# A conv and attention block in f32: position terms out of the first pair's front, second filters' steps held behind the first attention, cv1 and m2 ahead of the second projection

## The chip, the cores and the metric

The kernel runs on one core of a Trainium2 chip. The core has five engines that run side by side, each with its own list of instructions: PE (matmuls), DVE (VectorE, elementwise work), ACT (ScalarE, activations and copies), POOL (GpSimd, small elementwise work here and the issue of stores) and SP (which only issues DMA transfers, mostly loads). An engine takes its list strictly in order; an instruction that waits for a semaphore holds up everything behind it on the same engine. The metric is device time of one execution in microseconds, and the median over several executions is given.

## The reference

Eight images of 512 channels on 32 x 32 positions, all in float32. The block is a group norm, a 1x1 convolution, two bottleneck layers with a 3x3 convolution and self-attention, and a closing 1x1 convolution with a residual:

```python
def bot_attention(x, qkv_w, rw, rh):          # x: b, 256, 32, 32
    qkv = conv2d(x, qkv_w, 0).reshape(b, 3, HEADS, HD, hw)
    q, k, v = (qkv[:, 0], qkv[:, 1], qkv[:, 2])
    r = (rw + rh).reshape(1, HEADS, HD, hw)
    logits = jnp.einsum('bhdi,bhdj->bhij', q, k + r) * HD ** (-0.5)
    a = jax.nn.softmax(logits, axis=-1)
    return jnp.einsum('bhij,bhdj->bhdi', a, v)
...
t = cbs(x, cv1_w, cv1_bn, 0)                  # 1x1, 512 -> 512, BN, silu
ys = [t[:, :C], t[:, C:]]                     # y0, y1: 256 channels each
for i in range(N):                            # N = 2 layers
    yi = ys[-1]
    z = cbs(yi, m_cv1_w[i], m_cv1_bn[i], 1)   # 3x3
    z = bot_attention(z, m_qkv_w[i], m_rw[i], m_rh[i])
    z = silu(bn_eval(conv2d(z, m_cv2_w[i], 0), m_cv2_bn[i]))   # "m2"
    ys.append(yi + z)
return cbs(jnp.concatenate(ys, axis=1), cv2_w, cv2_bn, 0)
```

The input is group-normalised (32 groups) before this block, and the input is added to its result. The position term r is a sum of one vector per column (rw, 256 x 32) and one per row (rh, 256 x 32): 256 channels by 1024 positions once it is spread out. HD is 64, there are 4 heads.

## The kernel before

**Tiling and order.** Channels lie on partitions, 128 at a time (NM = 2 blocks for 256 channels, NX = 4 for 512), positions on the free axis in halves of 512. The images are taken in four pairs. For each pair: group norm and cv1 of both images, 3x3 convolution of layer 1 for both, then projection and attention of the first image, a transition in which the next image's cv1, the first image's m2 and the second image's projection are done, the attention of the second image, and the same again for layer 2; then cv2. Each pair also does the next pair's norm and cv1 in the shade of its attentions and transitions. Pair 0 multiplies the 1x1 layers plainly (`project_direct`, `conv1x1`), later pairs use Strassen blocks that pair 0 prepares.

**The 3x3 convolution** works on transformed tiles. `tiles_in` turns an image into v_in on DVE (w_ba, w_ec, w_rows, w_d, w_ab on the way), `conv3x3` multiplies them with transformed filters u, and the result is turned back. A filter for a block of output channels oc and of input channels k is made by `make_u`: raw taps are loaded (576 KB) into a spare image buffer (`load_raw`, tile ypad) or into `taps` (`load_taps`), then in three rounds DVE forms row sums in place (L406 to L412) and six u_new tiles per round (L424 to L429), ACT two more (L422, L423), and POOL stores them to DRAM (L433). `make_u` is a generator: each `next` takes one of its eight steps. The u_new tiles come from small rings of buffers (six for the early ones, ten for the late), so a step waits until an earlier store has landed. Layer 1's filters are made in the front; those of layer 2 are named (0,0,0) ... (1,1,1) by (oc, k, spare buffer). (0,0,0) is stepped behind the first attention, (0,1,1), (1,0,1), (1,1,1) after it: 16 steps ahead of the second attention, eight hooked into it (`hooks(NORM_B, range(8, 16), ...)`), which between them make the 24 steps.

**The front of pair 0** (about 0 to 135 us) loads and normalises two images, makes layer 1's filters and cv1 of both images, then v_in of both images for three rounds i (L528 to L575), then the convolution. A few matmuls make the position term: `make_r_early(0)` lets PE spread rw and rh with a unit matrix (L205, L208, tile r_ps), ACT copies it (L214), and SP stores it (tile r). `project_direct` loads it again (r_in, L811) and adds it to the keys when they leave PSUM (kr, L822). For layer 2 the same term is made by `make_r(1)` on POOL (L218 copy, L222 add, L226 store).

**The transition** between pair 0's attentions (224 to 303 us). On PE: cv1 of the next pair's first image (ps<-x,w: 8 matmuls for each of four output blocks; blocks 0 and 1 first), first half of the second image's projection (ps<-z,w_qkv: k and q), s_ps (the sums of the last softmax group over partitions, L1024), v of the projection (L833), m2 of the first image (m_ps, L1205), remaining cv1 blocks, second half of the projection. The softmax sums of the last group take a way round: s_ps on PE, s_row on ACT, a DRAM round trip by SP into sums_all, rc on DVE (L1067), another round trip into rs, and z scaled by it on DVE (L1079); m2's last products need that z. cv1's blocks go through y_half or ypad on ACT (silu, L476), m2's through t.

**What sets the order.** Instructions stand on each engine in an order that is fixed when the kernel is built: a list scheduler weighs the data dependences and the order in which the code was written, and `with tc.issue_after(ins)` holds back all that is written inside until `ins` stands in the order. Work is handed to the attention as a table `behind` of callbacks, keyed by softmax group g or (g, step), which are called as the attention's steps are written; NG = 4 is the end. `end` holds what closes an attention: `end.added` (the last sum of probabilities), `end.sums`, `end.spread`, `end.scale`. PSUM tiles for 1x1 products come from a ring of three (`ps_big`), and one is free again when ACT or DVE has read it.

Of the kernel before, what the change touches and what calls it, by code (L numbers as in the profile page):

```python
# [44 lines left out]
F32 = mybir.dt.float32  # L45
I32 = mybir.dt.int32
AF = mybir.ActivationFunctionType
ALU = mybir.AluOpType
# [4 lines left out]
P = 128  # L53
# [8 lines left out]
def kernel(  # L62
# [63 lines left out]
        return yp[:, 1 : F + 1].rearrange("p h c w -> p (h c w)")  # L126

    def load_raw(n, oc, k, yp):
        nc.sync.dma_start(
            inside(yp)[:, : 9 * P].rearrange("p (t o) -> p t o", o=P), m_cv1_w[n, ts(k, P), :, ts(oc, P)]  # L130
        )
        return inside(yp)
# [59 lines left out]
    def load_m2(n):  # L192
        nc.sync.dma_start(m2_sb[:, n], m_cv2_w[n].rearrange("(k p) o -> p k o", p=P))

    def make_r_early(n, raw):

        for c in range(NM):
            nc.scalar.copy(planes(rw_sb[:, n, c : c + 1]), natural(raw[:, c : c + 1]))
        ident = act.tile([P, P], F32, tag="h", name="ident", bufs=2)
        make_identity(nc, ident)  # L200
        for c in range(NM):
            ps = ps_big.tile([P, NH, HALF], F32, tag="big", name="r_ps")
            for half in range(NH):
                to = ps[:, half, :].rearrange("p (h w) -> p h w", w=F)
                nc.tensor.matmul(  # L205
                    to, ident, rw_sb[:, n, c].unsqueeze(1).to_broadcast([P, ROWS, F]), start=True, stop=False
                )
                nc.tensor.matmul(  # L208
                    to, ident, rh_sb[:, n, c, ts(half, ROWS)].unsqueeze(2).to_broadcast([P, ROWS, F]),
                    start=False, stop=True,  # L210
                )
            for half in range(NH):
                r = act.tile([P, HALF], F32, tag="t", name="r_new", bufs=4)
                nc.scalar.copy(r, ps[:, half, :])  # L214
                nc.sync.dma_start(r_dram[n][c][:, ts(half, HALF)], r)

    def make_r(n, raw):
        nc.gpsimd.tensor_copy(planes(rw_sb[:, n]), natural(raw))  # L218
        for c in range(NM):
            for half in range(NH):  # L220
                r = act.tile([P, ROWS, F], F32, tag="t", name="r_new", bufs=4)
                nc.gpsimd.tensor_tensor(  # L222
                    r, rw_sb[:, n, c].unsqueeze(1).to_broadcast([P, ROWS, F]),
                    rh_sb[:, n, c, ts(half, ROWS)].unsqueeze(2).to_broadcast([P, ROWS, F]), ALU.add,
                )
                nc.gpsimd.dma_start(r_dram[n][c][:, ts(half, HALF)], r.rearrange("p h w -> p (h w)"))  # L226
# [245 lines left out]
    def stages(act, small, ps_big, ps_av, n_pt):  # L472
# [330 lines left out]
        def project_direct(n, z, w, early=None, middle=None):  # L803
# [5 lines left out]
            for c in range(NM):  # L809
                rs.append(act.tile([P, HW], F32, tag="pt", name="r_in", bufs=n_pt))  # L810
                nc.sync.dma_start(rs[c], r_dram[n][c])  # L811

            def qk(c):
                for which in (1, 0):
                    o = which * C + c * P
                    ps = conv1x1(
                        lambda k: w[k][:, o : o + P], lambda k, half: z[:, k, ts(half, HALF)], NM
                    )
                    if which == 0:
                        nc.scalar.copy(q[:, c], ps.rearrange("p a b -> p (a b)"))  # L820
                    else:
                        tt(kr[:, c], ps.rearrange("p a b -> p (a b)"), rs[c], ALU.add)  # L822

            qk(0)
            if early:
# [659 lines left out]
    def putter(vs, g):  # L1485
        return lambda i, cp: vs[i, cp][:, :, g]
# [91 lines left out]
    for p in range(NP):  # L1578
# [70 lines left out]
            next(norm, None) if norm else None  # L1649

        def step_u():
            next(more_u, None)

        def begin_cv1(which, y1, b):
            def run():
# [24 lines left out]
        if p == 0:  # L1680
            q_tiles = [act.tile([P, 3 * C], F32, tag=tag, name="qkv_raw") for tag in ("p3", "p4")]
            load_qkv(1, q_tiles)
            q_sums = [act.tile([P, 2, 3, P], F32, tag=tag, name="sq_new") for tag in ("p1", "p2")]
            before = behind[3, 2]
            behind[3, 2] = lambda: (before(), make_sq(1, q_tiles, [t[:, j] for t in q_sums for j in range(2)]))
        end = s.attention_fast(qkv, z[:, :, 0], at_of(ia, 0), behind)
        for made in more_u:
# [9 lines left out]
                nc.gpsimd.dma_start(v_dram[i][cp], v_new.pop((i, cp)))  # L1697

        ec = {}
        if p == 0:  # L1700
            more_u = filters([(0, 1, 1), (1, 0, 1), (1, 1, 1)])

        def m2_a():
            return s.m2(0, z[:, :, 0], Y1[0], lambda oc, half: inner(Y2[0], oc, half))
# [20 lines left out]
            feed(units(1)[:6])  # L1725
            qkv = s.project_strassen(0, z[:, :, 1], take_blocks("sq", 0, 1, SQ_NAMES), t)
        else:
            if p == 0:
                with tc.issue_after(end.added.ins):
                    make_r(1, load_r(1, "acc", 2))  # L1730
            else:
                t = s.first_sum(z[:, :, 1])
            if more:
                nxt.go_on()

            def middle():
                end.spread()
                end.scale()
                m2_a()
                if more:  # L1740
                    for i in range(2, 4):
                        nxt.rest(i)
                    nxt.keep()
                s.exp_table()

            if not more:
                feed(units(1)[:6])
            if direct:
                qkv = s.project_direct(
                    0, z[:, :, 1], [take(key) for key in direct_keys(1)], early=end.sums, middle=middle  # L1750
                )
# [8 lines left out]
            store(i)  # L1760

        norm = None
        if p == 0:
# [13 lines left out]
        def parts_of(ocs):  # L1777
# [24 lines left out]
        for made in more_u:  # L1802
            pass
        if more:
            nxt.sums()
        vs = v_units()
# [29 lines left out]
        if p == 0:  # L1836
# [197 lines left out]
```

## Time and profile before

| | us |
|---|---|
| runs | 2362.28, 2359.41, 2361.51 (median 2361.51) |
| profiled execution, its own time | 2363.26 |
| its span on the core | 2361.7 |
| PE busy | 2239.6 (95%) |
| DVE busy | 1741.9 (74%) |
| ACT busy | 1087.8 (46%) |
| POOL busy | 211.8 (9%) |
| mean granted PE clock | 0.987 |

The profile is of one execution. Its page divides the span into 40 slices of 59 us, with one digit per slice for the busy share in tenths. A timeline line gives start, duration, engine, source line, operation, output<-inputs, shape and how many instructions were drawn together; in brackets stands the idle time of the engine just before it and the operation that ended the wait. `[5.41 <-ACT y_half L476]` reads: the engine stood for 5.41 us, and what let it go on was ACT's y_half of line 476. "x8" on PE counts records; one f32 matmul of 128 x 512 leaves two and takes 0.859 us when rows of them follow each other (27.63 us for 64 records, x_second). A window line gives, for a stretch from:to, its length, the busy time and instructions of PE, PEld, DVE, ACT and POOL, the granted PE clock, the DMA engines' mean share and the GB/s. A share may come out a little over 1.

Where pair 0 lies in the span: front 0 to 135, first attention 158 to 224, transition 224 to 303, second attention 303 to 374, layer 2's convolution from 409, its first attention 464 to 522. Pair 1's first transition, 824.17 to 874.68, takes 50.5 us; pair 0's takes 78.9.

### The profile page before, as it was taken

To read this page: it belongs to the slowest core of one execution; us is meant where nothing else is said; L and a number is where in the kernel's file an instruction comes from. 1 tells how busy PE (TensorE), PEld (TensorE's weight loads), DVE (VectorE), ACT (ScalarE), POOL (GpSimd) and SP (SyncE) were. 2 spreads that over 40 slices of the span, in tenths; PEclk is the share of its full clock that TensorE was granted. 3 is DMA by queue.
4 is the path that set the end of the run, shared out by engine and by line. 5 is a ranking of instruction groups with operands and counts; after the bars stand their busy time and mean duration, and the time that the engine had idled before them with its cause. 6 is when DMAs were issued, how large, how long until landed. Compare 5 with 4: busy or idle time off the path is not lost.

```text
span 2361.7 us, 40480 instructions
## 1 busy us (share of the span) xinstructions
PE 2239.6 (95%) x16354; PEld 1086.2 (46%) x16354; DVE 1741.9 (74%) x2626; ACT 1087.8 (46%) x1325; POOL 211.8 (9%) x416
## 2 busy tenths in 40 slices
PE   7798799999999999999999999999999999999997
PEld 3553333734447343744346444463344733373443
DVE  5967477877947878986775868887794777787642
ACT  6244254355323666355422565635522354335532
POOL 3103211000021000000022001000002100000002
PEclk9899899999999999999999999999999999999999
DMA  9522633631257051523147233351126711161114
GB/s 319 205 102 88 213 110 129 223 105 49 68 152 249 23 174 55 177 91 104 33 121 233 100 98 105 101 188 60 64 68 151 244 33 59 57 202 33 55 24 134
DMA packets 132930, 283.40 MB, mean 120 GB/s; under 512 B 34208, under 2 KB 60048, under 8 KB 131712
## 3 DMA queue, kind: packets, MB, share of 16 engines
q1 hardware_dynamic: 105712, 198.01, 25.7%
q0 software_dynamic: 27024, 82.72, 11.5%
q8 instruction: 131, 2.15, 0.4%
q14 instruction: 63, 0.52, 0.1%
HBM read 212.65 MB, written 68.03 MB: 119 GB/s over the span
## 4 chain that ended last, share of the span: by engine, by line
PE 54%; DVE 16%; issue 15%; DMA 5%; ACT 2%; POOL 1%; SPq 0%; DVEq 0%; ACTq 0%; POOLq 0%
PE av_ps L1007 13%; PE l_ps L973 12%; PE c L1225 5%; PE p_ps L863 5%; PE m_ps L1205 4%; PE c_new L1225 3%; PE x_ps L1325 3%; PE ps L502 2%; DVE acc L993 2%; PE c_ps L619 2%; DMA c_out<-in_x_dram 2%; PE pv_ps L869 2%; ACT pt L977 1%; DMA rs<-r_dram 1%; PE s_ps L1024 1%
## 5 line engine op out<-in xcount | busy, mean ns | idle before, releaser
L977 ACT ACTIVATE pt<-l_ps 128x1024 f32<-128x1024 f32 x512 | 495.7, 1023 | 345.9 <-PE l_ps L973 313.6
L993 DVE TENSOR_TENSOR acc<-acc,pt 128x1024 f32<-128x1024 f32 x384 | 471.9, 1229 | 90.1 <-ACT pt L977 66.8
L973 PE MATMUL l_ps<-q,kr 64*64 64x512 f32 x4096 | 490.9, 593 | 15.5 <-ACT pt L977 13.7
L1007 PE MATMUL av_ps<-pt,vT 64*64 64x512 f32 x4096 | 491.0, 597 | 10.2 <-DVE z L1015 7.9
L973 PEld LDWEIGHTS l_ps<-q,kr 64*64 64x64 f32 x4096 | 156.5, 133 | 289.6 <-issue 247.6
L1007 PEld LDWEIGHTS av_ps<-pt,vT 64*64 64x64 f32 x4096 | 155.8, 134 | 288.2 <-issue 240.0
L619 PE MATMUL c_ps<-v_in,u 128*64 128x128 f32 x4320 | 239.8, 273 | 5.5 <-issue 5.5
L619 PEld LDWEIGHTS c_ps<-v_in,u 128*64 128x64 f32 x4320 | 235.8, 137 | 13.1 <-issue 13.0
L1205 PE MATMUL m_ps<-z,m_sb 128*128 128x512 f32 x256 | 114.4, 600 | 3.5 <-DVE z L1079 3.5
L863 PE MATMUL p_ps<-t_z,sq 128*128 128x512 f32 x224 | 106.7, 597 | 7.8 <-DVE c_t L626 7.8
L991 DVE TENSOR_TENSOR acc<-pt 128x1024 f32<-128x1024 f32 x64 | 78.0, 1218 | 38.0 <-ACT pt L977 38.0
L624 ACT COPY c_m<-c_ps 128x512 f32<-128x512 f32 x48 | 28.1, 586 | 165.9 <-PE c_ps L619 105.2
L476 ACT ACTIVATE t<-m_ps,bh,sh 128x512 f32<-128x512 f32 x64 | 46.8, 775 | 98.7 <-PE m_ps L1205 98.3
L863 PE MATMUL p_ps<-z,sq 128*128 128x512 f32 x168 | 80.2, 604 | 8.2 <-ACT z L476 8.2
L1275 POOL DMA_DIRECT2D c_out<-in_x_dram x56 | 50.4, 975 | 310.4 <-ACT c_out L476 307.1
L1205 PEld LDWEIGHTS m_ps<-z,m_sb 128*128 128x128 f32 x256 | 48.6, 192 | 62.8 <-issue 54.6
L1079 DVE TENSOR_TENSOR z<-z,rs 128x512 f32<-128x512 f32 x64 | 44.8, 699 | 34.3 <-DMA rs<-r_dram 34.3
L537 POOL MEMSET w_rows<- 128x32 f32 x48 | 7.9, 164 | 649.6 <-PE s_ps L1024 377.0
L1015 DVE TENSOR_TENSOR z<-av_ps,z 128x512 f32<-128x512 f32 x64 | 43.9, 687 | 27.1 <-ACT z L1014 27.1
L476 ACT ACTIVATE z<-z,bh,sh 128x512 f32<-128x512 f32 x64 | 46.9, 803 | 30.1 <-DVE z L657 29.3
L476 ACT ACTIVATE c_out<-cz,bh,sh 128x512 f32<-128x512 f32 x14 | 16.7, 1293 | 91.1 <-DVE cz L1302 91.1
L863 PEld LDWEIGHTS p_ps<-t_z,sq 128*128 128x128 f32 x224 | 38.7, 190 | 39.9 <-issue 28.9
(313 smaller groups left out, 3200.0 us busy)
## 6 DMA issues: line engine op xcount, KB each, us to landing
u<-u SPq DMA_DIRECT2D x135, 512.0 KB
r_in<-r SPq DMA_DIRECT2D x32, 512.0 KB
sq<-sq SPq DMA_DIRECT2D x42, 384.0 KB
rs<-r_dram SPq DMA_DIRECT2D x120, 128.0 KB
x<-in_x_dram SPq DMA_DIRECT2D x28, 512.0 KB
y_in<-y SPq DMA_DIRECT2D x28, 512.0 KB
c_out<-in_x_dram POOLq DMA_DIRECT2D x56, 256.0 KB, 5.3
out_dram<-c_out POOLq DMA_DIRECT2D x56, 256.0 KB, 3.5
```

The costliest lines, as they stand in the source:

```text
L476: silued[0] = nc.scalar.activation(dst, src, AF.Silu, scale=sh[:, k : k + 1], bias=bh[:, k : k + 1])
L619: nc.tensor.matmul(to[o], us[cp][:, k, row, c, o], rhs, start=(k == 0), stop=(k == NM - 1),)
L863: nc.tensor.matmul(ps[:, o, :], w[:, o, :], rhs, start=not onto, stop=True, skip_group_check=onto)
L973: nc.tensor.matmul(ps[kh * HD : (kh + 1) * HD, hd, :], kr[r, c, o : o + HD], q[r, c, ts(half, HALF)], start=True, stop=True,)
L977: last_exp[0] = exp = nc.scalar.activation(pt, ps, AF.Exp, scale=SCALE)
L991: return nc.vector.tensor_tensor(accs[g], pt[0], pt[1], ALU.add)
L993: ins = nc.vector.tensor_tensor(accs[g], accs[g], pt[i], ALU.add)
L1007: nc.tensor.matmul(avs[g][hd * HD : (hd + 1) * HD, kh, :], vT[r, j, o : o + HD], pt[i][r, hd, :], start=(j == 0), stop=(j == NJ - 1),)
L1205: nc.tensor.matmul(pss[oc][:, half, :], m2_sb[:, n, k, ts(oc, P)], ao[:, k, ts(half, HALF)], start=(k == 0), stop=(k == NM - 1),)
L1225: nc.tensor.matmul(ps[:, o, :], w[:, k, ts(o, P)], rhs[part][:, c], start=(k == 0 and not onto), stop=(k == KB - 1), skip_group_check=onto,)
L1275: nc.gpsimd.dma_start(t, rows_of(x, i, at), accum_op=ALU.add)
L1325: nc.tensor.matmul(ps[:, o, :], w[:, c, ts(o, P)], rhs[c], start=(c == 0 and not onto), stop=(c == 1), skip_group_check=onto,)
```

## The change

1. The front no longer spreads layer 1's position term: `make_r_early` goes, and with it r_ps, the unit matrix, four ACT copies, four stores and the loads of r_in. `turn_r` only brings rw into its layout (two ACT copies). `project_direct` adds rw and then rh to the keys on DVE, broadcast from the small tiles.
2. The spread term of layer 1, which pair 1 needs, is made by POOL (`make_r(0, None)`) behind layer 2's first attention of pair 0. That of layer 2 (`make_r(1, ...)`) is written behind the first attention of layer 1 instead of after it.
3. `load_raw` for layer 2 is issued by POOL instead of SP.
4. In the front five steps of the filter (0,1) of layer 1, instead of two, stand ahead of the second image's averages.
5. The 24 steps of layer 2's filters (0,1,1), (1,0,1), (1,1,1) are held behind `end.added` of the first attention and all lie in the transition (5, 7, 3 and the remaining 9 steps, each part held behind the one before); none is hooked into the second attention.
6. The transition is written in another order for pair 0: sums, cv1 block 1, spread, steps, scale, m2, cv1 blocks 2 and 3, and only then the whole projection of the second image, so `early` and `middle` of `project_direct` are no longer used.

```diff
     def load_raw(n, oc, k, yp):
-        nc.sync.dma_start(
+        (nc.gpsimd if n else nc.sync).dma_start(
...
+    def turn_r(n, raw):
+        for c in range(NM):
+            nc.scalar.copy(planes(rw_sb[:, n, c : c + 1]), natural(raw[:, c : c + 1]))
...
-    def make_r_early(n, raw):
...
     def make_r(n, raw):
-        nc.gpsimd.tensor_copy(planes(rw_sb[:, n]), natural(raw))
+        if raw is not None:
+            nc.gpsimd.tensor_copy(planes(rw_sb[:, n]), natural(raw))
...
-            rs = []
-            for c in range(NM):
-                rs.append(act.tile([P, HW], F32, tag="pt", name="r_in", bufs=n_pt))
-                nc.sync.dma_start(rs[c], r_dram[n][c])
...
-                        tt(kr[:, c], ps.rearrange("p a b -> p (a b)"), rs[c], ALU.add)
+                        dst = img(kr[:, c])
+                        rw = rw_sb[:, n, c].unsqueeze(1).to_broadcast([P, F, F])
+                        rh = rh_sb[:, n, c].unsqueeze(2).to_broadcast([P, F, F])
+                        tt(dst, img(ps.rearrange("p a b -> p (a b)")), rw, ALU.add)
+                        tt(dst, dst, rh, ALU.add)
...
-    make_r_early(0, rw_raw)
     chunk = make_u(0, 1, 0, areas[0, 1, 0], new=u_new_early)
     with tc.issue_after(made.ins):
-        for _ in range(2):
+        for _ in range(5):
             made = next(chunk)
...
+    turn_r(0, rw_raw)
...
+            first = behind[1, 2]
+            raw_1 = load_r(1)
+            behind[1, 2] = lambda: (first(), make_r(1, raw_1))
...
-                with tc.issue_after(end.added.ins):
-                    make_r(1, load_r(1, "acc", 2))
...
             if direct:
-                qkv = s.project_direct(
-                    0, z[:, :, 1], [take(key) for key in direct_keys(1)], early=end.sums, middle=middle
-                )
+                more_u = filters([(0, 1, 1), (1, 0, 1), (1, 1, 1)])
+                end.sums()
+                nxt.go_on()
+                end.spread()
+                with tc.issue_after(end.added.ins):
+                    for _ in range(5):
+                        made = step_u()
+                with tc.issue_after(made.ins):
+                    end.scale()
+                    for _ in range(7):
+                        made = step_u()
+                last = m2_a()
+                with tc.issue_after(made.ins):
+                    for _ in range(3):
+                        made = step_u()
+                for i in range(2, 4):
+                    nxt.rest(i)
+                nxt.keep()
+                s.exp_table()
+                with tc.issue_after(made.ins), tc.issue_after(last.ins):
+                    for made in more_u:
+                        pass
+                feed(units(1)[:6])
+                qkv = s.project_direct(0, z[:, :, 1], [take(key) for key in direct_keys(1)])
...
-        if p == 0:
-            for _ in range(16):
-                step_u()
-            feed(units(1)[:6])
...
-        behind = hooks(NORM_B, range(8, 16), {1: lambda: tiles_later(2)}) | {
+        behind = hooks(NORM_B, (), {1: lambda: tiles_later(2)}) | {
...
-            behind[2] = lambda: make_sq(0, tiles, sums)
+            behind[2] = lambda: (make_sq(0, tiles, sums), make_r(0, None))
```

More of the change, by code (lines that the diff above doesn't have):

```diff
@@ L193, in load_m2 @@
         nc.sync.dma_start(m2_sb[:, n], m_cv2_w[n].rearrange("(k p) o -> p k o", p=P))
-    def make_r_early(n, raw):
-        for c in range(NM):
[L198 to L206, printed above, removed]
-                )
[L208 to L215, printed above, removed]
     def make_r(n, raw):
-        nc.gpsimd.tensor_copy(planes(rw_sb[:, n]), natural(raw))
+        if raw is not None:
+            nc.gpsimd.tensor_copy(planes(rw_sb[:, n]), natural(raw))
         for c in range(NM):
@@ L807, in project_direct @@
             vT = act.tile([P, NJ, C], F32, tag="v", name="vT")
-            rs = []
-            for c in range(NM):
-                rs.append(act.tile([P, HW], F32, tag="pt", name="r_in", bufs=n_pt))
-                nc.sync.dma_start(rs[c], r_dram[n][c])
             def qk(c):
@@ L1651, in step_u @@
         def step_u():
-            next(more_u, None)
+            return next(more_u, None)
         def begin_cv1(which, y1, b):
@@ L1699 @@
         ec = {}
-        if p == 0:
-            more_u = filters([(0, 1, 1), (1, 0, 1), (1, 1, 1)])
         def m2_a():
@@ L1727 @@
         else:
-            if p == 0:
-                with tc.issue_after(end.added.ins):
-                    make_r(1, load_r(1, "acc", 2))
-            else:
+            if not direct:
                 t = s.first_sum(z[:, :, 1])
-            if more:
-                nxt.go_on()
             def middle():
@@ L1739, in middle @@
                 m2_a()
[L1740 to L1743, printed above, removed]
                 s.exp_table()
@@ L1748 @@
             if direct:
-                qkv = s.project_direct(
-                    0, z[:, :, 1], [take(key) for key in direct_keys(1)], early=end.sums, middle=middle
-                )
+                more_u = filters([(0, 1, 1), (1, 0, 1), (1, 1, 1)])
[22 more added lines that the diff above has]
+                qkv = s.project_direct(0, z[:, :, 1], [take(key) for key in direct_keys(1)])
                 feed(cv1_keys(1))
@@ L1762 @@
         norm = None
-        if p == 0:
-            for _ in range(16):
-                step_u()
-            feed(units(1)[:6])
         tiles_later(1)
@@ L1801 @@
         end = s.attention_fast(qkv, z[:, :, 1], at_of(ib, 0), behind, at_once=True)
-        for made in more_u:
-            pass
         if more:
```

## The prediction

> **What bounds the kernel now.** I read the busy slices first, then a table of stretches, then PE's timeline inside the stretches that look thin.
>
> ```profile
> PE   7798799999999999999999999999999999999997
> PEclk9899899999999999999999999999999999999999
> ```
>
> Each digit is 59 us. PE is full from the seventh slice on; only the first six (0 to 354 us, pair 0) have room, and the granted clock dips in the same ones. All parts of the change lie there, so the rest of the 2361.7 us is left alone.
>
> ```profile
> 158.07:224.22 66.15, 59.85 (x546) 21.19 (x545) 52.73 (x71) 42.20 (x51) 14.96 (x19) 0.97 0.13 46
> 224.22:303.13 78.91, 62.01 (x156) 29.60 (x152) 40.05 (x85) 21.07 (x31) 19.01 (x36) 0.89 0.66 228
> 303.13:373.73 70.60, 62.19 (x546) 20.47 (x545) 55.59 (x79) 41.16 (x48) 7.39 (x14) 0.95 0.21 74
> 766.02:824.17 58.15, 57.68 (x546) 21.54 (x545) 49.73 (x65) 39.15 (x44) 3.68 (x5) 1.00 0.08 24
> 874.68:937.46 62.78, 58.12 (x546) 20.18 (x545) 54.37 (x72) 39.14 (x44) 4.04 (x8) 1.00 0.12 39
> ```
>
> Columns: stretch, length, busy PE, PEld, DVE, ACT, POOL, clock, DMA share, GB/s. Rows one to three are pair 0's first attention, the transition, and its second attention; the last two are pair 1's attentions, the same matmuls without filter steps: 8.0 and 7.8 us shorter.
>
> In the front (0 to 135 us) the last wait is not PE's own:
>
> ```profile
> 54.01 0.56 DVE L406 TENSOR_TENSOR ypad<-ypad 128x384 f32<-128x384 f32 x1 [10.57 <-DMA ypad<-in_m_cv_w_dram]
> ...
> 96.93 5.54 PE L619 MATMUL c_ps<-v_in,u_new 128*64 128x128 f32 x64 [5.87 <-DVE v_in L574]
> 110.03 9.30 PE L619 MATMUL c_ps<-v_in,u_new 128*64 128x128 f32 x128 [7.57 <-ACT c_m L624]
> ```
>
> PE waits for v_in, which DVE makes without a gap from 60 to 140 us (9.4 to 9.97 of each 10 us). DVE is late because it stood 10.57 us for the raw taps of filter (0,1,1), which layer 2 alone needs. **DVE bounds the front.**
>
> In the transition PE waits four times, 16.9 us together:
>
> ```profile
> 247.07 5.58 PE L502 MATMUL ps<-z,w_qkv 128*128 128x512 f32 x8 [5.41 <-ACT y_half L476]
> 258.49 1.08 PE L1024 MATMUL s_ps<-acc,ones 128*32 128x256 f32 x8 [5.84 <-ACT y_half L476]
> 261.71 8.55 PE L833 MATMUL p_ps<-w_qkv,z 128*128 128x256 f32 x32 [2.14 <-DVE kr L822]
> ...
> 281.50 3.68 PE L1205 MATMUL m_ps<-z,m_sb 128*128 128x512 f32 x4 [3.50 <-DVE z L1079]
> ```
>
> The first two are PSUM waits on ACT, which stands behind u_new copies waiting for DVE filter steps. The last ends the chain of softmax sums: s_ps at 258.49, z at 280.75, 22 us.
>
> **Front: the position terms and the held steps.** PE loses 8 r_ps matmuls, 42.25 to 49.13: 6.88 us. It is hidden today behind DVE, but brings the second image's cv1 forward, which must happen for DVE to profit. ACT loses four copies of 0.52 us, SP four r stores and two r_in loads of pair 0's first projection. DVE loses the 10.57 us stall and the three 0.56 us operations behind it (1.65 us): 12.2. Against that, its next steps need u_new buffers; their stores take 8.8 us (512 KB) to land at a DMA share of 1.06, so I estimate 2.6 us of new waits. Image 0's first w_ba moves from 70.26 to about 60.5. Image 1's w_ba needs its last silu (71.65 + 2.28 = 73.93, less 6.88 = 67.05) and follows image 0's 7.48 us of tiles at 68.0: from 77.74, 9.7 earlier. So v_in, and the conv behind it, come about 9.7 us earlier; PE is ready at 85.35 - 6.88 = 78.5. PE alone would give 6.9, DVE alone 12.2 - 2.6 = 9.6.
>
> Against it stands something the words of the change don't say: in the changed instruction order POOL makes r(1) here, among the u stores (source: behind the first attention), and the broadcast adds meet DVE's busiest stretch. The row for this is at the end of the first attention today:
>
> ```profile
> 215.41 3.44 POOL L222 TENSOR_TENSOR r_new<-rw_sb,rh_sb 128x512 f32<-128x512 f32 x2
> ...
> 216.41 1.54 DVE L1079 TENSOR_TENSOR z<-z,rs 128x512 f32<-128x512 f32 x1
> 217.87 1.26 DVE L424 TENSOR_TENSOR u_new<-ypad 128x256 f32<-128x256 f32 x1
> 219.97 4.62 DVE L993 TENSOR_TENSOR acc<-acc,pt 128x1024 f32<-128x1024 f32 x2
> ```
>
> Alone these take 0.69, 0.42 and 2.56: 3.8 us lost. The Trainium skill (SBUF — State Buffer, "Who interferes with whom") says why, and speaks against the move: a DVE instruction with two SBUF inputs and a GpSimd one that reads SBUF exclude one another, and the later one waits for the whole instruction. By the rule DVE could lose all of POOL's 3.44 + 2.06 + 1.26 (copy) = 6.8 us; by the row 3.8, and some of the front's DVE operations have one input. I take 2.2. Front: 9.7 - 2.2 = **7.5** (5 to 10.6).
>
> Load_raw of layer 2 moves from SP to POOL: two loads among the front's u stores, two in the transition. A DMA issue costs POOL 0.54 us; the same page's box on DMAs from GpSimd warns that DVE can starve them, but POOL's 256 KB u stores land in 5.4 us in this front, beside a busy DVE. By the row it costs nothing as long as the u stores behind it aren't waited for; at worst the 2 us that they would slip, in the range above.
>
> **First attention.** The r_new contention leaves: the 3.8 us on DVE were mostly slack, PE idles there 1 to 2 us a time. Gain **1** (0 to 3).
>
> **Transition.** PE's new order: cv1 8 matmuls, s_ps, cv1 8, m2 6, cv1 1 group, m2's rest, cv1, then the whole projection. Bare work: 56 matmuls of 0.859 us = 48.1, v 7.1, s_ps 0.6: 55.8 us, so at most 78.9 - 55.8 = 23 can go. s_ps starts at T0 + 7 instead of T0 + 34. Pair 1 does the same chain, uncongested, from s_ps 827.73 to z 839.64 in 12 us; today's took 22, at a DMA share of 0.96. PE needs the scaled z at about T0 + 21. In between, the filters: all 24 steps now lie here (16 before), on DVE (per filter 18 operations at 0.34 and six at 0.6 us from issue to issue: 9.7) 29 us, and rc stands on DVE behind the first operation of filter (1,0,1), which waits for its raw load on POOL. That load can start when filter (0,1,1) has read its taps (T0 + 15), lands 5 to 6 us later, rc follows at about T0 + 22 to 25, rs 5 us after (the 4.97 us row): z at T0 + 27 to 30, a PE wait of 6 to 9. With 2 us for the clock and PSUM waits: 55.8 + 7.5 + 2 = 65.3. Gain 13.6, taken as **13** (5 to 17; the lower end if ACT's y_half waits of 5.4 and 5.8 stay, since cv1's second and third group still need PSUM from an ACT that also copies u_new). The kr adds double to two of 1.2 us on DVE for each c; in the first projection DVE has 1.42 us of work from 140 to 145 and almost none to 155, and the q products run behind k's; in the transition they follow all m2 work: nothing, or 1.2 if DVE's steps run late.
>
> **Second attention.** Its 8 hooked steps leave. Today 70.60 with 8.4 us of waits; pair 1's row without steps is 62.78. Gain **7** (4 to 7.8).
>
> **r(0).** POOL now makes it behind layer 2's first attention (463.92 to 522.19, 58.27 us); by the row above 3.8 us of DVE there, in an attention with 10 us of DVE slack: cost **1** (0 to 3). It is first needed by pair 1.
>
> **Sum:** 7.5 + 1 + 13 + 7 - 1 = 27.5. The profiled execution took 2363.26 us, its span 2361.7; the median of the other runs, 2361.51, is within 0.1% of either. 2361.5 - 27.5 = **2334**.
>
> **Rivals.** (a) The front's gain is taken elsewhere: DMA is at 1.03 to 1.06 from 20 to 50 us, and if the u stores, not the raw load, are what DVE meets next, the stall is only renamed. For: a 5.08 us u wait exists at 249.87. Against: the stores after 52 us landed with DMA at 0.65. Then 20 us remain: **2342**.
> (b) The packed steps make DVE the transition's bound: 29 us of steps, some 20 of sq, z, m2, tiles, kr and statistics, two load waits of 6 and the u wait of 5 already seen come to 66, and it starts 5 us behind and ends in kr: 71 to 75 us. Transition gain 4, front 6.5, rest 7: 17 us, **2345**; with y_half's waits repeated, 2348.
> (c) Slower: the raw load stalls rc. In the front such a load took 37.2 to 54.0, 16.8 us. At that price z comes at T0 + 41, the transition is 78 us and gives nothing. The other gains are 14.5 us, so the kernel loses once z comes after T0 + 56: the load would also have to stand 15 us in POOL's queue behind u stores that wait for ACT. Two such waits: **2367**.
> (d) The change doesn't do what it says: r(1) isn't behind the attention but in the front, where by the rule (6.8) instead of the row it takes the front's gain to 3: **2339**.
>
> **Numbers.** Forecast 0.55; a 0.13, b 0.18, c 0.05, d 0.09. The low end takes the upper bound of each part (10.6 + 3 + 17 + 7.8: 38, 2323, and a few us below), the high end the lower ones (5 + 0 + 5 + 4 - 3: 11, 2350): 2320 to 2350. What a measurement can tell is about 0.2%, 4.7 us: faster 0.92, same 0.04, slower 0.04.
>
> **What would show it.** DVE without the 10 us wait at 43 us and the first conv matmul near 78; DVE rows stretched beside r_new before 80 us; s_ps 7 us after the last attention matmul; PE waiting once, 6 to 9 us, for the scaled z; second attention near 63; layer 2's conv starting 28 us before 409.5. Wrong if DVE waits on u stores at 45 to 55 us, if y_half's waits return, or if rc stands behind ypad for more than 10 us.

## The result and the profile after

| | before | after |
|---|---|---|
| median, us | 2362.3 | 2354.3 |
| ratio, 95% interval | | 0.9965 (0.9957 to 0.9973) |
| span of the profiled execution | 2361.7 | 2351.5 |
| last matmul ends | 2347.2 | 2334.2 |

Faster by 8 us, 0.35%, where 27.5 were forecast. The time lies outside the forecast's range (2320 to 2350). The gain by stage shows where the sum failed (starts and ends from PE's timelines):

| stage | before | after | gain | forecast |
|---|---|---|---|---|
| front, to the first attention | 158.07 | 155.76 | 2.3 | 7.5 |
| first attention | 66.15 | 66.14 | 0.0 | 1 |
| transition | 78.91 | 69.93 | 9.0 | 13 |
| second attention | 70.60 | 62.77 | 7.8 | 7 |
| layer 2's first attention | 58.27 | 64.27 | -6.0 | -1 |
| sum | | | 13.1 | 27.5 |

From there to the last matmul nothing changes (13.0). Behind it the profiled execution of before needs 14.5 us, that of the changed kernel 17.3; over all kernels below it is 11.3 to 17.3, with the same instructions, so I read it as scatter; why, stays open. With it, and with profiled times 1.0 us above and 1.3 below their medians, 13 becomes 8.

The two rows of busy slices and the table of stretches (length; busy PE, PEld, DVE, ACT, POOL; clock; DMA share; GB/s) of the changed kernel:

```profile
PE   7798899999999999999999999999999999999997
PEclk9899899999999999999999999999999999999999
```

```profile
155.76:221.90 66.14, 59.85 (x546) 21.20 (x545) 52.43 (x76) 42.20 (x51) 6.67 (x12) 0.97 0.11 39
221.90:291.83 69.93, 59.46 (x157) 28.18 (x153) 48.84 (x109) 22.34 (x35) 24.86 (x43) 0.90 0.79 283
291.83:354.60 62.77, 58.12 (x546) 20.16 (x545) 48.00 (x60) 40.16 (x45) 4.04 (x8) 1.00 0.14 51
444.79:509.06 64.27, 59.88 (x538) 20.08 (x537) 50.74 (x55) 35.09 (x40) 11.66 (x16) 0.95 0.29 100
```

The last row is layer 2's first attention, which was this before:

```profile
463.92:522.19 58.27, 57.35 (x538) 19.66 (x537) 48.13 (x55) 34.98 (x40) 4.31 (x8) 1.00 0.28 93
```

The second attention's clock is back at 1.00; layer 2's first attention is new trouble, with 11.66 us of POOL in it, where POOL's r(0) now stands, and a clock of 0.95. The front, from PE's and then DVE's timeline:

```profile
83.27 7.13 PE L603 MATMUL c_ps<-v_in,u_new 128*64 128x128 f32 x96 [4.04 <-DVE v_in L558]
94.65 5.36 PE L603 MATMUL c_ps<-v_in,u_new 128*64 128x128 f32 x64 [4.25 <-DVE v_in L558]
```

```profile
48.70 0.42 DVE L408 TENSOR_TENSOR u_new<-taps 128x256 f32<-128x256 f32 x1 [3.33 <-DMA u<-u_new]
...
55.72 2.80 DVE L408 TENSOR_TENSOR u_new<-taps 128x256 f32<-128x256 f32 x1 [2.15 <-DMA u<-u_new]
...
78.95 0.69 DVE L548 TENSOR_TENSOR w_d<-w_rows 128x512 f32<-128x512 f32 x1 [4.46 <-POOL w_rows L521]
```

PE is ready at 79.2, close to the 78.5 of the forecast, and DVE's 10.57 us for the raw taps is gone. But PE still waits for v_in: DVE now stands 5.7 us for u stores (3.33 and 2.15 in the rows above and 0.19 between them), loses 2.4 in one operation of 2.80 us (0.42 elsewhere), and stands 4.46 us for a memset of two tile columns that POOL does. POOL's timeline says why:

```profile
65.25 0.18 POOL L521 MEMSET w_rows<- 128x32 f32 x1
65.31 0.18 POOL L522 MEMSET w_rows<- 128x32 f32 x1
65.39 11.00 POOL L206 TENSOR_TENSOR r_new<-rw_sb,rh_sb 128x512 f32<-128x512 f32 x2
76.34 1.09 POOL L210 DMA_DIRECT2D r<-r_new  x2
77.42 0.76 POOL L237 DMA_DIRECT2D sq<-qkv_raw  x1
78.17 0.56 POOL L1440 DMA_DIRECT2D y<-ypad  x1
78.74 0.18 POOL L521 MEMSET w_rows<- 128x32 f32 x1
```

Two adds that take 2.06 us at 56 us took 11.00 beside DVE's tiles, and the memset for the next tiles stood behind them and four DMA issues. DVE's own operations in those 11 us were not stretched. Taken one by one, the first add took 9.99 us and the second 1.04. The first ended at 75.4, 0.9 us after DVE had come to a stop at 74.5, and an undisturbed add takes 1.06: by these times it got through only when DVE stood still, and DVE stood still because its memset was behind that add. In three variants below that leave the front alone (r0_late, chain_first, steps_back) the same add took 9.98 to 10.00 us.

In the transition PE now waits twice, from the timelines of PE, DVE and ACT:

```profile
247.68 2.08 PE L486 MATMUL ps<-x,w 128*128 128x512 f32 x2 [5.87 <-ACT y_half L460]
254.36 3.78 PE L1189 MATMUL m_ps<-z,m_sb 128*128 128x512 f32 x4 [4.60 <-DVE z L1063]
```

```profile
241.04 0.56 DVE L390 TENSOR_TENSOR ypad<-ypad 128x384 f32<-128x384 f32 x1 [5.95 <-DMA ypad<-in_m_cv_w_dram]
```

```profile
244.76 0.42 ACT L406 ACTIVATE u_new<-ypad 128x256 f32<-128x256 f32 x1 [3.06 <-DVE ypad L392]
...
245.38 2.25 ACT L460 ACTIVATE y_half<-ps,bh,sh 128x512 f32<-128x512 f32 x2
```

The scaled z came a little later than forecast (31.7 us after the stage's start, against 27 to 30). The y_half wait did not go. Behind the DVE line stood the next filter's steps; ACT's u_new copies waited for them, and y_half stood behind those copies on ACT.

In layer 2's first attention, DVE, then PE, and PE at the same place in the kernel before:

```profile
486.47 3.21 DVE L977 TENSOR_TENSOR acc<-acc,pt 128x1024 f32<-128x1024 f32 x2
489.78 1.88 DVE L977 TENSOR_TENSOR acc<-acc,pt 128x1024 f32<-128x1024 f32 x1
493.57 2.20 DVE L975 TENSOR_TENSOR acc<-pt 128x1024 f32<-128x1024 f32 x1
```

```profile
493.80 0.93 PE L1008 MATMUL s_ps<-acc,ones 128*32 128x256 f32 x8 [2.68 <-DVE acc L977]
496.43 3.69 PE L991 MATMUL av_ps<-pt,vT 64*64 64x512 f32 x16 [1.71 <-DVE z L999]
```

```profile
511.73 1.95 PE L1007 MATMUL av_ps<-pt,vT 64*64 64x512 f32 x16 [0.92 <-DVE z L1015]
```

A pair of acc alone takes 2.56, one 1.22. POOL's r_new runs from 487.55 to 494.69 and these are late just where a softmax group ends: PE needs the last acc for s_ps. It waits 2.68 and 1.71 us, where before it waited 0.92: 3.5 us of the 6.0. The rest is the clock: the 16 records behind take 3.69 us, 1.95 before.

### The profile page after: what moved, and what is told of

The parts are those of the page before. It is cut to its first block, busy times and chain, and to the rows that moved or that the text cites. A ratio compares the mean times of both kernels' runs of the same rounds, so it can differ in the third digit from the quotient of the medians.

```text
span 2351.5 us, 40448 instructions
## 1 busy us (share of the span) xinstructions
PE 2231.2 (95%) x16338; PEld 1083.4 (46%) x16338; DVE 1745.9 (74%) x2630; ACT 1085.3 (46%) x1321; POOL 229.6 (10%) x426
## 3 DMA queue, kind: packets, MB, share of 16 engines
q8 instruction: 131, 2.15, 0.4%
## 4 chain that ended last, share of the span: by engine, by line
PE 58%; issue 16%; DVE 14%; DMA 4%; ACT 2%; POOL 1%; SPq 0%; DVEq 0%; ACTq 0%; POOLq 0%
PE av_ps L991 13%; PE l_ps L957 12%; PE c L1209 7%; PE c_new L1209 5%; PE m_ps L1189 4%; PE p_ps L847 4%; PE ps L486 3%; PE c_ps L603 3%; PE x_ps L1309 3%; DVE acc L977 2%; PE pv_ps L853 2%; ACT pt L961 1%; PE s_ps L1008 1%; DMA rs<-r_dram 1%; DVE c_e L611 1%
## 5 line engine op out<-in xcount | busy, mean ns | idle before, releaser
L991 PEld LDWEIGHTS av_ps<-pt,vT 64*64 64x64 f32 x4096 | 155.2, 134 | 285.4 <-issue 240.8
L486 PE MATMUL ps<-x,w 128*128 128x512 f32 x128 | 57.8, 606 | 5.9 <-ACT y_half L460 5.9
```

The source lines that it names most:

```text
L486: last_product[0] = nc.tensor.matmul(ps[:, half, :], w_of(k), rhs_of(k, half), start=(k == begin), stop=(k == end))
L991: nc.tensor.matmul(avs[g][hd * HD : (hd + 1) * HD, kh, :], vT[r, j, o : o + HD], pt[i][r, hd, :], start=(j == 0), stop=(j == NJ - 1),)
```

## The experiments

All lie between the changed kernel and variants of it; what was expected stands ahead of each result. Times are stage lengths in us from PE's timeline; the two rows that say "starts" and the one that says "ends" are points in time; the ratio is to the kernel before.

| | after | r1_back | r0_late | r_both | raw_sp | chain_first | steps_back | rest_only | best | best2 | at_once |
|---|---|---|---|---|---|---|---|---|---|---|---|
| first attention starts | 155.8 | 148.6 | 155.2 | 148.7 | 151.8 | 155.9 | 155.7 | 154.7 | 147.7 | 148.2 | 148.0 |
| first attention | 66.1 | 69.0 | 66.1 | 68.9 | 66.5 | 66.5 | 65.6 | 65.7 | 66.2 | 67.4 | 66.1 |
| transition | 69.9 | 72.2 | 69.8 | 70.2 | 69.2 | 65.2 | 70.9 | 74.7 | 63.8 | 64.9 | 64.9 |
| second attention | 62.8 | 63.3 | 62.9 | 63.6 | 62.8 | 63.1 | 71.3 | 62.8 | 63.6 | 63.6 | 63.6 |
| layer 2, first attention | 64.3 | 64.4 | 61.0 | 59.3 | 61.7 | 64.5 | 63.0 | 59.0 | 58.7 | 58.7 | 58.9 |
| pair 1, first projection | 21.4 | 21.4 | 23.1 | 22.7 | 21.4 | 21.4 | 21.1 | 21.4 | 24.6 | 21.4 | 21.4 |
| pair 1, second attention starts | 861.1 | 858.7 | 859.7 | 855.4 | 853.8 | 856.3 | 868.3 | 859.0 | 845.8 | 844.9 | 845.6 |
| last matmul ends | 2334.2 | 2335.8 | 2334.1 | 2330.2 | 2329.3 | 2329.6 | 2345.0 | 2333.6 | 2319.6 | 2320.1 | 2322.5 |
| ratio | 0.9965 | 0.9947 | 0.9972 | 0.9943 | 0.9937 | 0.9951 | 1.0008 | 0.9960 | 0.9896 | 0.9869 | 0.9866 |

The intervals are about 0.0015 to either side (0.0008 to 0.0010 for after, r0_late and steps_back); so two columns are clearly apart only from about 0.002 on. They come from four rounds, each beside its own runs of the kernel before, whose medians went from 2360.9 to 2366.2. From pair 1's second attention to the last matmul all execute the same code, in 1473.1 to 1477.1 us: up to 4 us between two ends are scatter, and the row of pair 1's second attention shows better what an edit was worth.

**r1_back**: layer 2's term out of the front.

```diff
-            first = behind[1, 2]
-            raw_1 = load_r(1)
-            behind[1, 2] = lambda: (first(), make_r(1, raw_1))
...
+                with tc.issue_after(end.added.ins):
+                    make_r(1, load_r(1, "acc", 2))
                 end.sums()
```

> Layer 2's position term goes back to its place of before (the end of the first attention); all else as changed. Theory: in the front the changed kernel lost 6.9 us to POOL's r_new, 4.46 us in which DVE waited for a w_rows memset queued behind r_new and 2.4 us in one stretched DVE operation. Then the first attention starts at 149 to 151 us instead of 155.76, the first attention stays at 66 us, and the whole is about 5 us faster than the changed kernel (2349, ratio 0.9943). Rival: the front is held by u_new buffers whose stores have not landed (3.33 and 2.15 us of DVE waits) and the 4.46 us only turn into another wait: attention starts at 154 or later and the time stays within 2 us of the changed kernel.

```profile
79.23 5.46 PE L603 MATMUL c_ps<-v_in,u_new 128*64 128x128 f32 x96
```

The first attention starts at 148.6, 7.2 us earlier: the front's loss was r_new. PE no longer waits for the first v_in. DVE's waits for u stores stay, at 3.31, 0.17 and 1.65 us; the memset wait is gone. But the first attention grew to 69.0 and the transition to 72.2, and of 7.2 us 2.4 are left at pair 1's second attention (858.7); the last matmul ends no earlier, and the ratio of 0.9947 says some 4 us, at the edge of the noise of both. The first attention's growth isn't r_new's, as r_both shows.

**r0_late**: layer 1's term from layer 2's attention to the closing convolution of pair 0.

```diff
-            behind[2] = lambda: (make_sq(0, tiles, sums), make_r(0, None))
+            behind[2] = lambda: make_sq(0, tiles, sums)
...
             b3(bottom)
+            if p == 0:
+                make_r(0, None)
```

> Layer 1's position term is made by POOL in pair 0's closing convolution instead of behind layer 2's first attention; all else as changed. Theory: r_new beside DVE's sums of probabilities made that attention 64.27 us long instead of 58.27; it returns to 58.3 us, and the whole is 6 us faster than the changed kernel (2348, ratio 0.994). Rival: the attention is longer for another reason (buffers or DMA timing after the new transition): it stays at 62 us or more and the time doesn't move.

The attention falls to 61.0, not 58.3: r_new held 3.3 of the 6 us. DVE's additions are no longer stretched; PE's two waits are 0.84 and 1.00 us, and most of what is left is the clock, 0.97 over the attention (r_both below has waits of 0.91 and 1.01 us, a clock of 1.00 and 59.3 us). In the order that was built POOL makes r(0) at 712 to 726 us, not in the closing convolution but in pair 1's first convolution, and pair 1's first projection loses 1.7 us (23.1). At pair 1's second attention 1.4 us are left, and the whole did not move: the theory missed the total.

**r_both**: r(1) beside m2 ahead of layer 2's convolution, r(0) as in r0_late.

```diff
         s.tiles_in(Y2[0], putter(vs, 0), [0])
+        if p == 0:
+            make_r(1, load_r(1))
         last = s.m2(0, z[:, :, 1], Y1[1], lambda oc, half: inner(Y2[1], oc, half))
```

> Layer 2's position term is made beside m2 and cv1 ahead of layer 2's convolution, layer 1's in pair 0's closing convolution, both on POOL; neither stretch leaves PE waiting in the changed kernel. Theory: both losses go, first attention from about 150 us, layer 2's first attention 58.3 us: about 12 us faster than the changed kernel, 2342, ratio 0.9915. Rival: the front keeps its loss in another wait (2348, 0.994), or the stretch ahead of layer 2's convolution gets the same lock and loses 3 to 6 us itself.

The front's gain is there (148.7), and layer 2's attention takes 59.3. But r(1) did not land where the code has it. POOL makes it at 332 to 337 us, inside the second attention (287.8 to 351.4), again at the end of a softmax group:

```profile
333.92 5.24 DVE L977 TENSOR_TENSOR acc<-acc,pt 128x1024 f32<-128x1024 f32 x2 [0.86 <-ACT pt L961]
```

The pair of additions takes 2.55 us in the changed kernel. DVE loses 2.7 us and PE 0.8 of them, as a new wait of 0.84 us for acc (attention 63.6 instead of 62.8; the same in best), since DVE stands 1.31 us for ACT behind that pair in the changed kernel and could make up for the rest. The first attention has 68.9 us without any r_new in it. PE's waits are those of the changed kernel, 6.4 us against 6.3; the difference is the clock. The same ten microseconds of the attention's end, r_both first, the changed kernel below:

```profile
200.00:210.00 10.00, 7.07 (x44) 2.05 (x48) 6.15 (x8) 7.26 (x10) 1.15 (x4) 0.66 0.08 28
```

```profile
207.00:217.00 10.00, 7.22 (x68) 2.41 (x72) 7.13 (x9) 8.84 (x11) 1.41 (x4) 1.00 0.08 28
```

Waits of 1.90 and 1.37 us (r_both) and 1.62 and 1.58 us (changed) give a granted clock of 0.66 in the one and 1.00 in the other, and 44 records done instead of 68. The length of the waits doesn't decide it: in raw_sp, below, they are 1.90 and 1.59 us, and the clock is 1.00:

```profile
203.00:213.00 10.00, 6.85 (x64) 2.26 (x68) 6.76 (x9) 9.21 (x12) 1.15 (x4) 1.00 0.08 28
```

**raw_sp**: layer 2's raw loads on SP.

```diff
-        (nc.gpsimd if n else nc.sync).dma_start(
+        nc.sync.dma_start(
             inside(yp)[:, : 9 * P].rearrange("p (t o) -> p t o", o=P), m_cv1_w[n, ts(k, P), :, ts(oc, P)]
```

> Layer 2's raw filter loads go back to SP's queue; all else as changed. Theory (the queue change is worth nothing by itself): transition 69 to 71 us, front within 1 us, time within 2 us of the changed kernel (2354, ratio 0.9965). Rival: POOL's queue is what delays the raw load in the transition (5.95 us of DVE wait, with the softmax reciprocal behind it), then the transition gets 3 to 5 us shorter; or SP's loads come back so late in the front that DVE waits there.

The transition is the same (69.2): POOL's queue is not what delays the raw load there. The front gains 4 us, which neither theory had. SP issues the two loads at 32 to 42 us, POOL had at 19.8 and 32.7, and DVE's first wait for u stores falls from 3.33 to 0.42 us. But the later ones grow (0.26, 2.26, 0.62 and 1.58 us), 5.1 us together instead of 5.7, and DVE begins image 0's tiles at 63.6 instead of 64.1. What went is the memset wait of 4.46 us, as r_new fell otherwise: three of the four adds were done by 58.4, and one stood ahead of the memset (DVE's stretched operations cost 3.1 us there, 2.4 in the changed kernel).

```profile
65.94 5.37 POOL L206 TENSOR_TENSOR r_new<-rw_sb,rh_sb 128x512 f32<-128x512 f32 x1
```

So most of the 4 us is r_new's cost once more. With r_new out of the front (r_both against best) the queue is worth 1.0 us there.

**chain_first**: in the transition, filter (0,1,1)'s last steps behind ACT's s_row, filter (1,0,1)'s behind rc (`noted` keeps the two instructions).

```diff
                 with tc.issue_after(made.ins):
                     end.scale()
-                    for _ in range(7):
-                        made = step_u()
+                    with tc.issue_after(end.noted["row"].ins):
+                        for _ in range(3):
+                            made = step_u()
+                with tc.issue_after(made.ins), tc.issue_after(end.noted["rc"].ins):
+                    for _ in range(4):
+                        made = step_u()
```

> As the changed kernel, but in the transition the steps of filter (0,1,1) that need ACT stand behind ACT's s_row copy, and those of filter (1,0,1) behind the reciprocal rc, so that the chain of softmax sums waits neither for u_new copies nor for a raw load. Theory: the transition's two PE waits (5.87 us for ACT's y_half, 4.60 us for the scaled z) both come from that order; both shrink to under 2 us each and the transition goes from 69.9 to 61 to 65 us, the whole 5 to 8 us under the changed kernel (2348, ratio 0.994). Rival: the DMA round trips of the sums set the scaled z by themselves, or the y_half wait comes from the u_new buffers: the transition stays at 67 to 70 us and the time within 3 us of the changed kernel.

```profile
243.62 1.12 PE L487 MATMUL ps<-x,w 128*128 128x512 f32 x2 [1.30 <-ACT y_half L460]
249.58 3.78 PE L1191 MATMUL m_ps<-z,m_sb 128*128 128x512 f32 x4 [4.84 <-DVE z L1064]
```

The theory held for one wait, the rival for the other: the y_half wait was the steps' order (5.87 to 1.30), the z wait was not (4.84). From s_row to rc pass 9.3 us and from rc to z 6.1, the two DRAM round trips. The transition is 65.2, near the 65.3 of the prediction.

**steps_back**: the last eight steps hooked into the second attention again.

```diff
                 with tc.issue_after(made.ins), tc.issue_after(last.ins):
-                    for made in more_u:
-                        pass
+                    made = step_u()
...
-        behind = hooks(NORM_B, (), {1: lambda: tiles_later(2)}) | {
+        behind = hooks(NORM_B, range(8, 16), {1: lambda: tiles_later(2)}) | {
```

> As the changed kernel, but the last eight filter steps are hooked into the second attention again. Theory: the second attention goes from 62.8 back to about 70.6 us and the transition shortens by no more than 2 us, as its last steps lie beside full PE work: 5 to 8 us slower than the changed kernel (2361, ratio 0.999). Rival: the eight steps cost the transition as much as the attention: both change by 5 us or more and the time stays within 2 us of the changed kernel.

The second attention is 71.3, the transition 70.9, the whole 2362.9: no faster than before. The eight steps cost the attention 8.5 us and, taken out of the transition, save it nothing.

**rest_only**: the kernel before with parts 5 and 6 alone. Against the changed kernel these lines of before are back, among others (the raw loads on SP, the loads of r_in, no r(0) behind layer 2's attention):

```diff
+    make_r_early(0, rw_raw)
...
-        for _ in range(5):
+        for _ in range(2):
             made = next(chunk)
...
+                with tc.issue_after(end.added.ins):
+                    make_r(1, load_r(1, "acc", 2))
...
-                        tt(dst, img(ps.rearrange("p a b -> p (a b)")), rw, ALU.add)
-                        tt(dst, dst, rh, ALU.add)
+                        tt(kr[:, c], ps.rearrange("p a b -> p (a b)"), rs[c], ALU.add)
```

> The kernel before with parts 5 and 6 of the change alone (filters' steps held behind the first attention, new order of the transition); the position terms, the queue of the raw loads and the front's two steps stay as before. Theory: transition near 70 us and second attention near 63 us as in the changed kernel, layer 2's first attention at 58.3 us, and the front as fast as the changed kernel's or faster, since what parts 1 to 4 give there (6.9 us of PE) is taken back by POOL's r_new: 2342 to 2345, ratio 0.9925, at least as fast as the whole change. Rival: parts 1 to 4 carry the change, and without them the first attention starts at 158 us and the transition is longer: 2352 or more.

0.9960: as fast as the whole change. The front starts its attention at 154.7 with all of `make_r_early` in it; parts 1 to 4 added nothing on balance. But the transition is 74.7, with waits for y_half (3.49, 2.39) and z (7.52); why they are longer there was not tried. And the front's stall was renamed, though not to u stores as rival (a) had it: DVE's 10.57 us for the raw taps became 7.76 us for ACT's u_new, ACT being busy all that time with the second image's norm and four r_new copies (2.1 us). Whether the copies or the order of part 4 makes that wait was not separated. It costs little here: PE reaches the first convolution product at 85.2 without a wait for v_in, with the r_ps matmuls ahead of it.

**best**: r_both, raw_sp and chain_first together, their edits as shown.

> The changed kernel with all four corrections: layer 2's position term made ahead of layer 2's convolution, layer 1's in the closing convolution, raw loads on SP, and the chain of softmax sums ahead of the filters' steps as in chain_first. If they add up: 17.9 us by the best of the earlier ones' stages and 5 to 8 us of the transition: 2338 to 2342, ratio 0.9905. If the chain's order gives nothing, 2347, ratio 0.9935.

2336.25, 0.9896 (0.9879 to 0.9913). At pair 1's second attention it is 15.3 us ahead of the changed kernel; the three alone are 5.7, 7.3 and 4.8 ahead, 17.8 together. They nearly add up; what is missing lies in the front, where 8.0 us come of 7.1 and 4.0, both being mostly r_new.

**best2**: best, with r(0) written earlier, ahead of the second image's first products of the closing convolution.

```diff
+            if p == 0:
+                make_r(0, None)
             b1()
             b1_more()
...
             b3(bottom)
-            if p == 0:
-                make_r(0, None)
```

> As the kernel with all four corrections, but layer 1's position term stands earlier in the closing convolution of pair 0, ahead of the second image's first products. Theory: in that kernel POOL made it so late (697 to 713 us) that DVE was held at the end of pair 1's first convolution and pair 1's first projection took 24.6 us instead of 21.4; made earlier it costs nothing: 2333 us, ratio 0.988, that projection at 21.4 us. Rival: the projection waits for something else, or the add now collides with the closing convolution's tiles: no change, 2336, 0.9895.

In best POOL made r(0) at 697 to 713 us, in pair 1's first convolution; here at 644 to 658, in the closing convolution, each add in 1.05 us. Pair 1's first projection, best first:

```profile
718.58 3.45 PE L848 MATMUL p_ps<-t_z,sq 128*128 128x512 f32 x4 [3.10 <-DVE c_t L611]
```

```profile
718.88 1.95 PE L848 MATMUL p_ps<-t_z,sq 128*128 128x512 f32 x4 [1.18 <-DVE c_t L611]
```

The projection is at 21.4 us. The last matmul does not end earlier (2320.1, 2319.6): 2.3 us were lost ahead of it in the first attention and the transition, which the edit does not touch (in the attention by the clock: 0.66 from 198 to 208 us, with waits of 2.17 and 0.53 us). Median 2335.8, ratio 0.9869 (0.9852 to 0.9885). That is best's median; the ratio is lower because the kernel before was slower in that round (2366.2 against 2360.9), and the two intervals touch.

**at_once**: best2, the first attention's last sums kept on the chip; chain_first's hold now stands behind the scaled z instead of rc.

```diff
+        if p == 0:
+            behind[NG + 1] = lambda: nxt.go_on()
-        end = s.attention_fast(qkv, z[:, :, 0], at_of(ia, 0), behind)
+        end = s.attention_fast(qkv, z[:, :, 0], at_of(ia, 0), behind, at_once=(p == 0))
...
-                end.sums()
-                nxt.go_on()
-                end.spread()
...
-                    end.scale()
...
-                with tc.issue_after(made.ins), tc.issue_after(end.noted["rc"].ins):
+                with tc.issue_after(made.ins), tc.issue_after(end.scaled.ins):
                     for _ in range(4):
                         made = step_u()
                 last = m2_a()
+                with tc.issue_after(last.ins):
+                    end.check()
```

> As best2, but the first attention's last softmax sums stay on the chip (PE spreads them over the partitions, DVE takes the reciprocal of 128x512 numbers), as the second attention does it, instead of two DRAM round trips. Theory: the 4.84 us that PE still waits for the scaled z are the two round trips (8.8 us from s_row to rc, 5.9 us from rc to z); they go and the transition shortens by 2 to 5 us: 2330, ratio 0.987. Rival: ACT's copies and DVE's reciprocal of the wide tile stand behind filter steps and z comes no earlier, or m2, now ahead, waits in another place: within 2 us of best2, or slower.

```profile
233.91 2.84 PE L1189 MATMUL m_ps<-z,m_sb 128*128 128x512 f32 x6 [0.28 <-DVE z L1063]
265.47 6.71 PE L817 MATMUL p_ps<-w_qkv,z 128*128 128x256 f32 x16 [4.66 <-DVE kr L805]
```

z comes at once (0.28 us instead of 4.61), and the wait turns up at the projection: kr stands on DVE behind filter steps and tiles, among them a new reciprocal of 3.35 us. It starts 50.0 us into the stage, in best2 48.5. Transition 64.9 as in best2; no gain. DVE, busy for 44.2 of those 50.0 us, is now what bounds that stage.

## Why the prediction failed, point by point

**Front (7.5, got 2.3).** PE's side was right (8 matmuls gone, ready at 79), and the stall of 10.57 us went. The step that failed is the price of r_new, taken as 2.2 us of stretched DVE operations by the row of the first attention. It cost 7.2 (r1_back), in DVE's rows 6.9: 2.4 of stretch, and 4.46 in which DVE waited for a memset queued behind r_new. That the tiles wait for POOL was in the code and the trace of before (w_rows at 71.89, 77.15); I counted DVE's loss to the lock, and not what stands behind r_new on its own queue. The waits for u buffers were sized too small as well (2.6 forecast, 5.7 measured), but that is not what was missing: r1_back keeps 5.1 us of them and its front is 9.5 us ahead of before, near the 9.7 worked out without r_new.

**First attention (1, got 0).** Its waits are for ACT's pt and DVE's statistics (1.08, 2.01, 1.62, 1.58), the same before and after; r_new at its end had been slack.

**Transition (13, got 9.0).** The order and s_ps came as worked out, z nearly 2 us late. The sum of 65.3 had no y_half wait in it, a term set to nothing and put at the lower end of the range; one of 5.87 us stayed, by the steps' order. chain_first takes it to 1.30 and the stage to 65.2.

**Second attention (7, got 7.8)** was right, and steps_back shows that the eight steps are all of it.

**r(0) (-1, got -6.0).** The step "10 us of DVE slack in the attention" failed: the slack is an average, and at the end of a group PE waits for the last acc. It lost 3.5 us in waits and the rest by the clock that fell behind them (0.95, before 1.00). With r_new there the attention takes 61.7 to 64.5 us over the runs, without it 58.7 to 61.0; r0_late against the changed kernel puts 3.3 on r_new, and some 2 us more go with the clock, which is at 0.95 to 0.97 in those with r_new and in r0_late, and at 1.00 in the others.

Of the rivals, (d) named the right place and took the front down to 3; that r(0) costs the same kind again at a second place was missing. (b) did not come: DVE is 48.84 of 69.93 us busy. (a) holds in a part, the u waits of 5.7 us, which r1_back shows to cost the front little. (c) did not come: the raw load in the transition held DVE for 5.95 us. r_new's two prices were wrong by 10 us together, the y_half wait by 4: nearly all of the 14.4 us between the forecast and the stages.

## What to carry to other kernels

A long instruction on a side engine is priced twice: by what it slows on the other engine, and by what waits behind it on its own queue; the second was the larger here. Slack over a stage says nothing of the few microseconds where a result is due. The same work at another place cost 0.8 us (r(1) in the second attention) or nothing that shows (r(0) early in the closing convolution). Where the code writes it is not where it executes: three times here r landed a stage away from its lines, so the trace has to say where. Corrections of place, queue and order alone made 0.35% into 1.0 to 1.3%.

## What the hardware showed that I had not expected

The exclusion between POOL's r_new and DVE fell on one side or the other. At 56 us two r_new took 2.06 us and DVE's operation 2.80 instead of 0.42; at 65 us two r_new took 11.00 and DVE's operations were not stretched; in layer 2's attention both lost. The Trainium skill (SBUF — State Buffer, "SBUF: two separate sides") gives the shared ports to whichever of the two starts first, for its whole instruction. The rows don't show that rule at work: by its record DVE's operation starts at 55.72, 0.44 us ahead of the first r_new, and still ends behind the second; and the add of 9.99 us would have to lose to one DVE operation after another. Who gets the ports next when both wait is not shown here.

The granted clock doesn't follow from the length of the waits: 0.66 against 1.00 for waits of the same size, 2.8 us in one attention. The skill (TensorE: Matmul & The Clock Gate, Part 1) says that the gate watches a free-running window, so that the place of a wait in it would decide; that fits, though no trace shows the window. A stage can lose 1 to 3 us when an earlier one gets shorter, as in r1_back, r_both and best2.
